# A two-block attention kernel: ternary weight pieces loaded and stored from ScalarE, and all seven quarters of the context kept in memory

## The chip, the cores and the metric

The kernel runs on one core of one Trainium2 chip. The metric is device time in microseconds (us) of one execution; lower is better. A core has five engines with a queue of instructions each: PE (TensorE, matrix products), DVE (VectorE), ACT (ScalarE), POOL (GpSimd) and SP (SyncE, here used for nothing but issuing DMAs). Semaphores hold an instruction back until what it needs is there, and what stands behind it in the same queue waits as well. On-chip data lie in SBUF (128 partitions) and in PSUM, into which PE writes its products. "In memory" below means DRAM outside both.

## The reference, cut to what matters

Eight sequences (B = 8) of 64 tokens of width 512 pass through two blocks. Each block lets the tokens attend to their sequence's context of 1601 rows of width 512, then to each other, then passes them through a feed-forward network; `n` is a layer norm. In short:

```python
x = x + cross_attention_0(n(x), ctx)      # 16 heads of 64, weights Wq, Wkv, Wout
x = x + spectral_attention_0(n(x))
x = x + moe_ffn_0(n(x))                   # 8 experts
x = x + cross_attention_1(n(x), ctx)      # 16 heads, weights Wq, Wk, Wv, Wp
x = x + attention_1(n(x))
x = x + ternary_ffn_1(n(x))
```

A cross attention is, for each sequence and head, `softmax(q @ k.T) @ v` with q from the tokens and k and v from the context. Block 0's is computed with the key weights multiplied onto the queries and the value weights applied after the mixing, so that the context itself stands in both large products. In the last network the two weight matrices (512x2048 and 2048x512) are rounded to three values, with one scale for each matrix:

```python
scale = 1.0 / clip(mean(abs(w)), 1e-05)
q = clip(round(w * scale), -1.0, 1.0) / scale
```

## The kernel before, in words

**The stages.** The program does block 0's cross attention (`l0_xattn`, 0 to about 1517 us of the span), its spectral attention, its experts (about 1600 to 1855), block 1's cross attention (`l1_xattn`, about 1855 to 2900), and block 1's attention with the ternary network (`l1_tail`, to the end). The change touches `l0_xattn`, a load in `l1_xattn`, and the class `TernaryWeights`, which the program makes ahead of the first stage.

**Order of instructions.** The kernel is written in one thread of program text. A scheduler of the language spreads it over the engines' queues and may move an instruction ahead of others of the same engine; the order in a queue is therefore not always that of the text. Buffers come from pools with a fixed number of copies, and a DMA into a buffer waits until the last reader of its former content is done.

**Block 0's cross attention.** It goes through 17 steps (the loop at L648). Step 2b + half does the scores of sequence b for eight of the 16 heads (`scores`, products at L468), and after them the mixing of the context rows by the weights of the step before (`attend`, products at L585, then v at L618). Scores need the context transposed, `ctxT`; mixing needs it by rows, `ctx`. Both are taken in six "pairs" of two tiles of 128 context rows; the last 65 rows are a tail, done apart (L461, L595). Every fourth step ends with `project_out` (L640).

**Seven products in place of eight.** A pair and its counterpart form a 2x2 block product, which is done in seven products on sums and differences of quarters. For the context's side, `Quarters.left` (L132 to L139) makes four such sums on POOL; a pair is therefore a tile of seven quarters, 128 x 7 x 256 f32 (917 KB), of which three hold plain quarters of the input and four the sums. `LEFT` says which quarter a product takes. All pairs, of scores and of mixing, come from one pool of six buffers (`cp`, tag "pair"), and the output weights in `project_out` use it as well. `Run.add` writes out the order of the seven products of one pair among those of the pair before, over the PSUM tags x, y and z with two buffers each; ACT copies the products p1, u2 and p5 out of PSUM (L428 in scores) and writes one sum with the bias (L447), DVE makes the other sums (L433). `softmax` works on DVE (L501, L508 to L515) and ACT (L502), while PE does the next scores.

**Loads and kept quarters.** `load_columns(b, keep)` loads the six pairs of ctxT for a step, each with two DMAs of 256 KB from the input (L183), and makes the four sums. In the first half of each sequence it also writes the four sums of each pair into DRAM tiles `kept[b]` (L189, 128 KB, and L190, 384 KB). In the second half the same quarters are loaded from the input again and the sums made again. `load_rows` loads ctx, also two DMAs a pair (L200). All these DMAs are issued by SP.

**Block 1's cross attention.** Its helper `load(b, g)` (L1430 to L1445) loads one group of two pairs (1.8 MB): from the input the plain quarters (two DMAs a pair), from `kept` the four sums (two DMAs a pair), so eight DMAs for a group, all from SP. The weight of its output projection is loaded at L1596, on SP too.

**The ternary weights.** They are cut into 16 pieces of 512 KB. `pass_by` (L1881) loads one into a buffer "piece" (two buffers). `measure` sums its absolute values on ACT (L1889); `scales` makes the two scales (L1893 to L1898); `round` loads the piece again, scales it and adds a constant that rounds (DVE, L1904), subtracts the constant on ACT with a bf16 result in a buffer "wq" (L1905, one buffer), clips it on DVE (L1906), and stores it to memory from SP (L1907), from where `l1_tail` loads it at the end of the program. In the program's text `aside(step)` (L363) measures two pieces at the end of each of the steps 2 to 9, makes the scales in step 10 and rounds three pieces at the end of each of the steps 10 to 15. In the trace the measures stand at 239 to 450 us and the rounds at 1015 to 1151 us.

Of the kernel before, what the change touches and what calls it, by code (L numbers as in the profile page):

```python
# [10 lines left out]
F32 = mybir.dt.float32  # L11
BF16 = mybir.dt.bfloat16
# [8 lines left out]
P = 128  # L21
# [102 lines left out]
class Quarters:  # L124
# [5 lines left out]

    LEFT = {1: 0, 2: 1, 3: 6, 4: 3, 5: 4, 6: 5, 7: 2}

    @staticmethod
    def left(nc, q):

        nc.gpsimd.tensor_add(q[:, 4, :], q[:, 2, :], q[:, 3, :])  # L136
        nc.gpsimd.tensor_sub(q[:, 5, :], q[:, 4, :], q[:, 0, :])
        nc.gpsimd.tensor_sub(q[:, 2, :], q[:, 0, :], q[:, 2, :])
        nc.gpsimd.tensor_sub(q[:, 6, :], q[:, 1, :], q[:, 5, :])  # L139


def l0_xattn(K, x, d, ternary, kept):
# [7 lines left out]
    with ExitStack() as es:  # L150
# [25 lines left out]

        def load_columns(b, keep=False):

            pairs = []
            for i in range(NPAIR):  # L180
                q = cp.tile([P, 7, QH], F32, tag="pair", name="ctxT")
                for j in range(2):
                    nc.sync.dma_start(  # L183
                        q[:, ds(2 * j, 2), :].rearrange("p h (c n) -> p (h c) n", n=P),
                        d["ctxT"][b, :, ts(2 * i + j, P)].rearrange("(c p) n -> p c n", p=P),
                    )
                Quarters.left(nc, q)
                if keep:
                    nc.sync.dma_start(kept[b][:, i, 3, :], q[:, 2, :])  # L189
                    nc.sync.dma_start(kept[b][:, i, 0:3, :], q[:, 4:7, :])  # L190
                pairs.append(q)
            return pairs

        def load_rows(b):

            pairs = []
            for i in range(NPAIR):
                q = cp.tile([P, 7, QH], F32, tag="pair", name="ctx")
                for j in range(2):
                    nc.sync.dma_start(  # L200
                        q[:, 0:4, :].rearrange("p (h j) n -> p j h n", j=2)[:, j],
                        d["ctx"][b, ts(2 * i + j, P), :].rearrange("p (h n) -> p h n", n=QH),
                    )
                Quarters.left(nc, q)
                pairs.append(q)
            return pairs
# [103 lines left out]
        load_tails(0)  # L310
        ctxT = load_columns(0, True)
        place = [tp.tile([P, 4, 3, QH], F32, tag="pt", name="stage").rearrange("p a b q -> p (a b q)") for _ in range(2)]
# [138 lines left out]
        def scores(b, qkt, ctxT):  # L451
# [12 lines left out]
            for i in range(NPAIR):  # L464

                def mul(ps, n, start, i=i):
                    for e in range(2):
                        nc.tensor.matmul(  # L468
                            ps,
                            lhsT=ctxT[i][:, Quarters.LEFT[n], ts(e, P)],  # L470
                            rhs=right[n][:, e, :],
                            start=start and e == 0,
                            stop=e == 1,
                            skip_group_check=not start,
                        )
# [94 lines left out]
        def attend(half, s, soft, ctx, o, first):  # L570
# [77 lines left out]
        for step in range(2 * B + 1):  # L648
            if step < 2 * B:
                b, half = divmod(step, 2)  # L650
                if step:
                    now, ctxT = queries_of(b, half), load_columns(b, half == 0)
# [749 lines left out]
def l1_xattn(K, x, d, ahead, queries_done, in_last, kept):  # L1402
# [7 lines left out]
    with ExitStack() as es:  # L1410
# [19 lines left out]
        def load(b, g):  # L1430

            q = cp.tile([P, 2, 7, QH], F32, tag="ctxT", name="ctxT")
            for u in range(2):
                i = 2 * g + u
                nc.sync.dma_start(
                    q[:, u, 0:2, :].rearrange("p h (c n) -> p (h c) n", n=P),
                    d["ctxT"][b, :, ts(2 * i, P)].rearrange("(c p) n -> p c n", p=P),
                )
                nc.sync.dma_start(
                    q[:, u, 3, :].rearrange("p (c n) -> p c n", n=P),  # L1440
                    d["ctxT"][b, SET:, ts(2 * i + 1, P)].rearrange("(c p) n -> p c n", p=P),
                )
                nc.sync.dma_start(q[:, u, 2, :], kept[b][:, i, 3, :])
                nc.sync.dma_start(q[:, u, 4:7, :], kept[b][:, i, 0:3, :])
            return q  # L1445
# [413 lines left out]
class TernaryWeights:  # L1859
# [26 lines left out]

    def measure(self, piece, i):
        w = self.pass_by(piece, i)
        self.nc.scalar.activation(w, w, AF.Abs, accum_out=self.part[:, i // 8, i % 8 : i % 8 + 1])  # L1889
# [9 lines left out]

    def round(self, piece, pool, i):  # L1900
        nc, n = self.nc, i // 8
        w = self.pass_by(piece, i)
        q = pool.tile([P, 1024], BF16, tag="wq", name="wq")
        nc.vector.tensor_scalar(w, w, self.scale[:, n : n + 1], MAGIC, ALU.mult, ALU.add)  # L1904
        nc.scalar.activation(q, w, AF.Identity, bias=self.down, scale=1.0)  # L1905
        nc.vector.tensor_scalar(q, q, 1.0, -1.0, ALU.min, ALU.max)  # L1906
        nc.sync.dma_start(self.to[i], self.shaped(q, i))  # L1907

# [493 lines left out]
```

## Time and profile before

| | |
|---|---|
| times of the three runs | 3087.1, 3088.03, 3089.5 us (median 3088.03) |
| the profiled execution | 3083.06 us, of which the span 3081.1 |
| mean granted PE clock of it | 0.987 |
| PE busy | 2980.5 us |
| POOL's sums of ctxT pairs, one of four lines (L136) | 96, mean 823 ns |
| a measure on ACT (L1889) | 1.06 us and 0.19 us for its sum |
| a round: DVE L1904, ACT L1905, DVE L1906 (medians) | 0.75, 1.15, 0.43 us |
| load of a piece, issue to landing (median) | 4.3 us |
| store of a rounded piece, issue to landing (median) | 3.6 us |

The profile is that of one execution. Busy shares are of the whole span. A row of the waits gives the waiting engine with its tile and line, what ended the wait, the total, how often, and the longest one. A row of a timeline gives the start, the duration, the engine, the line and the operation; "SPq" is SP's queue, where a row is the issuing of a DMA, not its transfer, and "x6" folds six of them into one row. "Granted clock" is the share of its full clock that PE was given in a stretch.

### The profile page before, as it was taken

To read this page: it belongs to the slowest core of one execution; us is meant where nothing else is said; L and a number is where in the kernel's file an instruction comes from. 1 tells how busy PE (TensorE), PEld (TensorE's weight loads), DVE (VectorE), ACT (ScalarE), POOL (GpSimd) and SP (SyncE) were. 2 spreads that over 40 slices of the span, in tenths; PEclk is the share of its full clock that TensorE was granted. 3 is DMA by queue.
4 is the path that set the end of the run, shared out by engine and by line. 5 is a ranking of instruction groups with operands and counts; after the bars stand their busy time and mean duration, and the time that the engine had idled before them with its cause. 6 is when DMAs were issued, how large, how long until landed. Compare 5 with 4: busy or idle time off the path is not lost.

```text
span 3081.1 us, 41104 instructions
## 1 busy us (share of the span) xinstructions
PE 2980.5 (97%) x15515; PEld 2288.4 (74%) x15521; DVE 1830.5 (59%) x3124; ACT 845.5 (27%) x1620; POOL 993.0 (32%) x959
## 2 busy tenths in 40 slices
PE   8999999999999989999999999999999999999887
PEld 7777778888888767888654446778788888888654
DVE  4845545666656656666433333578676676676746
ACT  2322241222222322222111222232332333323234
POOL 4434343544454534444110003221422413304000
PEclk9999999999999999999999999999999999999998
DMA  8265474434434564432659974302112022020260
GB/s 263 71 200 152 145 244 128 140 100 143 131 103 132 180 188 134 128 119 66 228 185 339 343 253 144 92 15 75 42 51 77 21 73 58 22 89 3 87 107 14
DMA packets 387187, 391.76 MB, mean 127 GB/s; under 512 B 55054, under 2 KB 289558, under 8 KB 385838
## 3 DMA queue, kind: packets, MB, share of 16 engines
q1 hardware_dynamic: 380761, 371.80, 39.2%
q10 hardware_dynamic: 5589, 15.24, 1.3%
q8 instruction: 123, 2.02, 0.3%
q0 software_dynamic: 640, 2.10, 0.2%
q14 instruction: 74, 0.61, 0.1%
HBM read 332.90 MB, written 56.16 MB: 126 GB/s over the span
## 4 chain that ended last, share of the span: by engine, by line
PE 58%; DVE 2%; ACT 1%; DMA 1%; issue 0%; POOL 0%; POOLq 0%; ACTq 0%; DVEq 0%; SPq 0%
PE x_ps L1528 11%; PE y_ps L1528 8%; PE s_ps L1691 6%; PE oe_ps L1231 4%; PE h_ps L1204 4%; PE acc L1742 3%; PE x_ps L585 3%; PE x_ps L468 2%; PE z_ps L585 2%; PE z_ps L468 1%; PE sum_ps L1575 1%; PE y_ps L585 1%; PE y_ps L468 1%; DMA wo<-in_L1x_Wp 1%; PE vt_ps L1619 1%; PE top_ps L1727 1%
## 5 line engine op out<-in xcount | busy, mean ns | idle before, releaser
L1588 POOL TENSOR_TENSOR r<-r,minus_half 128x52 f32<-128x52 f32 x32 | 276.9, 8673 | 558.0 <-DVE r L1587 558.0
L468 PE MATMUL x_ps<-qt,ctxT 128*128 128x256 f32 x1152 | 288.1, 384 | 9.6 <-ACT u L428 6.9
L585 PE MATMUL x_ps<-pt,ctx 128*128 128x256 f32 x1152 | 281.7, 382 | 7.2 <-DVE a L561 6.3
L468 PEld LDWEIGHTS x_ps<-qt,ctxT 128*128 128x128 f32 x1152 | 218.7, 192 | 50.4 <-ACT u L428 8.8
L585 PEld LDWEIGHTS x_ps<-pt,ctx 128*128 128x128 f32 x1152 | 217.3, 190 | 41.1 <-DVE a L561 6.5
L136 POOL TENSOR_TENSOR ctxT<-ctxT 128x256 f32<-128x256 f32 x96 | 79.0, 823 | 412.4 <-DMA ctxT<-in_ctxT 284.5
L1691 PE MATMUL s_ps<-qb,kT 128*128 128x256 f32 x832 | 201.2, 381 | 0.1
L449 DVE TENSOR_TENSOR m<-m,s 128x512 f32<-128x512 f32 x176 | 137.5, 781 | 95.8 <-ACT s L447 93.2
L136 POOL TENSOR_TENSOR ctx<-ctx 128x256 f32<-128x256 f32 x96 | 73.5, 765 | 348.5 <-DMA ctx<-in_ctx 275.4
L1691 PEld LDWEIGHTS s_ps<-qb,kT 128*128 128x128 f32 x832 | 154.2, 190 | 26.2 <-issue 3.5
L501 DVE TENSOR_TENSOR s<-s,top_ps 128x1024 f32<-128x1024 f32 (+1 forms) x112 | 123.2, 1135 | 23.3 <-PE top_ps L491 23.3
L1733 DVE TENSOR_TENSOR s<-s,top_ps 128x1792 f32<-128x1792 f32 x64 | 117.9, 1884 | 28.8 <-PE top_ps L1727 28.8
L433 DVE SCALAR_TENSOR_TENSOR s<-y_ps,bias,p 128x256 f32<-128x256 f32 x96 | 46.3, 483 | 146.2 <-PE y_ps L468 145.8
L1701 DVE TENSOR_TENSOR s<-s_ps,r 128x512 f32<-128x512 f32 x192 | 126.4, 682 | 10.8 <-PE s_ps L1691 10.2
L1734 ACT ACTIVATE s<-s 128x1792 f32<-128x1792 f32 x64 | 101.0, 1591 | 84.0 <-DVE s L1733 84.0
L1742 PEld LDWEIGHTS acc<-s,v 128*64 128x64 f32 x1664 | 96.1, 138 | 32.4 <-issue 27.0
L502 ACT ACTIVATE s<-s 128x1024 f32<-128x1024 f32 (+1 forms) x112 | 110.8, 996 | 30.0 <-DVE s L501 25.9
L1742 PE MATMUL acc<-s,v 128*64 128x128 f32 x1664 | 114.9, 280 | 4.1 <-ACT s L1734 4.1
L1204 PE MATMUL h_ps<-w,tok 128*128 128x512 f32 x256 | 117.3, 593 | 0.0
L1231 PE MATMUL oe_ps<-w,hT 128*128 128x512 f32 x256 | 115.6, 593 | 0.0
L515 DVE TENSOR_TENSOR total<-total,s 128x512 f32<-128x512 f32 x160 | 110.0, 687 | 3.5
L468 PE MATMUL x_ps<-qk,ctxT 128*128 128x256 f32 x384 | 104.9, 391 | 6.2 <-ACT s L447 4.0
(472 smaller groups left out, 6287.2 us busy)
## 6 DMA issues: line engine op xcount, KB each, us to landing
w<-in_L0f_W SPq DMA_DIRECT2D x64, 1024.0 KB, 5.8
ctxT<-in_ctxT SPq DMA_DIRECT2D x240, 256.0 KB, 4.7
ctx<-in_ctx SPq DMA_DIRECT2D x192, 256.0 KB, 3.4
kept<-ctxT SPq DMA_DIRECT2D x48, 384.0 KB, 2.8
ctxT<-kept SPq DMA_DIRECT2D x48, 384.0 KB
wvT<-in_L0x_WvT SPq DMA_DIRECT2D x16, 1024.0 KB, 8.4
qk<-qk_all SPq DMA_DIRECT2D x15, 1024.0 KB, 7.4
qk_all<-stage SPq DMA_DIRECT2D x32, 384.0 KB, 3.5
```

Of the source, the lines that this page charges most:

```text
L136: nc.gpsimd.tensor_add(q[:, 4, :], q[:, 2, :], q[:, 3, :])
L449: nc.vector.tensor_max(self.m, self.m if k else self.s[:, LAST, :], self.s[:, k, :])
L468: nc.tensor.matmul(ps, lhsT=ctxT[i][:, Quarters.LEFT[n], ts(e, P)], rhs=right[n][:, e, :], start=start and e == 0, stop=e == 1, skip_group ...
L501: nc.vector.tensor_sub(s[:, k : k + n], s[:, k : k + n], top.unsqueeze(1).to_broadcast([P, n, HALF]))
L585: nc.tensor.matmul(ps, lhsT=ctx[pair][:, Quarters.LEFT[n], ts(m, P)], rhs=right[n][:, i, :], start=start and i == 0, stop=i == 2, skip_gro ...
L1204: nc.tensor.matmul(ps, lhsT=self.tok[:, c, :], rhs=self.w1[n][:, c, :], start=c == 0, stop=c == DC - 1)
L1231: nc.tensor.matmul(ps, lhsT=self.hT[:, f, :], rhs=self.w2[f // 4][:, f % 4, :], start=f == 0, stop=f == 15)
L1528: nc.tensor.matmul(ps, lhsT=left(n, e), rhs=right(n, e), start=start and e == 0, stop=e == 1, skip_group_check=not start,)
L1588: nc.gpsimd.tensor_tensor(r, r, minus_half, ALU.pow)
L1691: nc.tensor.matmul(ps[:, i].rearrange("p h q -> p (h q)"), lhsT=kT[c][:, ts(k0 + i, P)], rhs=qb[c].rearrange("p h q -> p (h q)"), start=Tr ...
L1701: nc.vector.tensor_mul(out, ps, by)
L1742: nc.tensor.matmul(acc[ds(64 * j, 64), c, :], lhsT=v[:, k, ds(c * P + 64 * j, 64)], rhs=s[:, k, ts(j, P)], start=k == 0, stop=k == NK - 1,)
```

## The change

There are three edits.

1. In `l0_xattn`, `kept` holds all seven quarters of a pair. In the first half of a sequence the pairs are loaded and summed as before and then stored whole, one DMA a pair (917 KB), issued behind the loads of all six pairs. In the second half a pair is one DMA from `kept`, with no sums on POOL. `load_rows` splits its two DMAs by the halves of the columns and no longer by the two tiles of rows. The places of the quarters in a tile are renumbered (`LEFT`, `left`).
2. In `l1_xattn`, a group of two pairs is one DMA of 1.8 MB from `kept`.
3. The ternary pieces are loaded and stored by DMAs that ACT issues. The work on them becomes a generator, `of_weights`, started after step 3, of which `scores` and `attend` take one turn after each `run.add`: two loads, three turns with nothing, two measures, and so on; later two loads, four turns with nothing, two rounds. Rounding is done in the piece's own buffer: two f32 operations on DVE (scale and upper bound; lower bound and rounding constant), then ACT writes bf16 over the same buffer and issues the store.

```diff
-    LEFT = {1: 0, 2: 1, 3: 6, 4: 3, 5: 4, 6: 5, 7: 2}
+    LEFT = {1: 5, 2: 6, 3: 2, 4: 4, 5: 0, 6: 1, 7: 3}
...
-        def load_columns(b, keep=False):
+        def load_columns(b, half=0):
             pairs = []
             for i in range(NPAIR):
                 q = cp.tile([P, 7, QH], F32, tag="pair", name="ctxT")
-                for j in range(2):
-                    nc.sync.dma_start(
-                        q[:, ds(2 * j, 2), :].rearrange("p h (c n) -> p (h c) n", n=P),
-                        d["ctxT"][b, :, ts(2 * i + j, P)].rearrange("(c p) n -> p c n", p=P),
-                    )
-                Quarters.left(nc, q)
-                if keep:
-                    nc.sync.dma_start(kept[b][:, i, 3, :], q[:, 2, :])
-                    nc.sync.dma_start(kept[b][:, i, 0:3, :], q[:, 4:7, :])
+                if half:
+                    nc.sync.dma_start(q, kept[b][:, i])
+                else:
+                    for j in range(2):
+                        nc.sync.dma_start(
+                            q[:, ds(5 - 2 * j, 2), :].rearrange("p h (c n) -> p (h c) n", n=P),
+                            d["ctxT"][b, :, ts(2 * i + j, P)].rearrange("(c p) n -> p c n", p=P),
+                        )
+                    Quarters.left(nc, q)
                 pairs.append(q)
+            if not half:
+                for i, q in enumerate(pairs):
+                    nc.sync.dma_start(kept[b][:, i], q)
             return pairs
...
-        def aside(step):
-            if 2 <= step < 10:
-                for i in range(2):
-                    ternary.measure(piece, 2 * (step - 2) + i)
-            if step == 10:
-                ternary.scales(ps_m.tile([P, 16], F32, tag="mm", name="w_ps"), ones[:, 0:1])
-            if 10 <= step < 16:
-                for i in range(3 * (step - 10), min(3 * (step - 9), 16)):
-                    ternary.round(piece, zp, i)
+        def of_weights():
+            for i in range(0, ternary.PIECES, 2):
+                pieces = [ternary.pass_by(piece, i + j) for j in range(2)]
+                yield from (None,) * 3
+                for j in range(2):
+                    ternary.measure(pieces[j], i + j)
+                    yield
+            ternary.scales(ps_m.tile([P, 16], F32, tag="mm", name="w_ps"), ones[:, 0:1])
+            for i in range(0, ternary.PIECES, 2):
+                pieces = [ternary.pass_by(piece, i + j) for j in range(2)]
+                yield from (None,) * 4
+                for j in range(2):
+                    ternary.round(pieces[j], i + j)
+                    yield
+        aside = iter(())
...
                 run.add(mul, Scores(s, m, b, i))
                 some(2)
+                next(aside, None)
...
                     run.add(mul, Mixed(a, m, part == 0, tail))
                     some(2 * part)
+                    next(aside, None)
...
-            aside(step)
             if step == 3:
                 some(5 * NG)
+                aside = of_weights()
...
+        for _ in aside:
+            pass
...
         def load(b, g):
             q = cp.tile([P, 2, 7, QH], F32, tag="ctxT", name="ctxT")
-            for u in range(2):
...
+            nc.sync.dma_start(q, kept[b][:, ts(g, 2)])
             return q
...
     def pass_by(self, piece, i):
         w = piece([D], "wraw").rearrange("p a b -> p (a b)")
-        self.nc.sync.dma_start(self.shaped(w, i), self.from_[i])
+        self.nc.scalar.dma_start(self.shaped(w, i), self.from_[i])
         return w
...
-        q = pool.tile([P, 1024], BF16, tag="wq", name="wq")
-        nc.vector.tensor_scalar(w, w, self.scale[:, n : n + 1], MAGIC, ALU.mult, ALU.add)
+        q = w.bitcast(BF16)[:, :1024]
+        nc.vector.tensor_scalar(w, w, self.scale[:, n : n + 1], 1.0, ALU.mult, ALU.min)
+        nc.vector.tensor_scalar(w, w, -1.0, MAGIC, ALU.max, ALU.add)
         nc.scalar.activation(q, w, AF.Identity, bias=self.down, scale=1.0)
-        nc.vector.tensor_scalar(q, q, 1.0, -1.0, ALU.min, ALU.max)
-        nc.sync.dma_start(self.to[i], self.shaped(q, i))
+        nc.scalar.dma_start(self.to[i], self.shaped(q, i))
...
-        kept = [memory.tile([P, NPAIR, 4, QH], F32, tag=f"kept{b}", name="kept") for b in range(B)]
+        kept = [memory.tile([P, NPAIR, 7, QH], F32, tag=f"kept{b}", name="kept") for b in range(B)]
```

More of the change, by code (lines that the diff above doesn't have):

```diff
@@ L124 @@
 class Quarters:
-    LEFT = {1: 0, 2: 1, 3: 6, 4: 3, 5: 4, 6: 5, 7: 2}
+    LEFT = {1: 5, 2: 6, 3: 2, 4: 4, 5: 0, 6: 1, 7: 3}
     @staticmethod
     def left(nc, q):
[L136 to L139, printed above, removed]
+        nc.gpsimd.tensor_add(q[:, 0, :], q[:, 3, :], q[:, 4, :])
+        nc.gpsimd.tensor_sub(q[:, 1, :], q[:, 0, :], q[:, 5, :])
+        nc.gpsimd.tensor_sub(q[:, 3, :], q[:, 5, :], q[:, 3, :])
+        nc.gpsimd.tensor_sub(q[:, 2, :], q[:, 6, :], q[:, 1, :])
 def l0_xattn(K, x, d, ternary, kept):
@@ L198, in load_rows @@
                 q = cp.tile([P, 7, QH], F32, tag="pair", name="ctx")
-                for j in range(2):
+                for h in range(2):
                     nc.sync.dma_start(
-                        q[:, 0:4, :].rearrange("p (h j) n -> p j h n", j=2)[:, j],
-                        d["ctx"][b, ts(2 * i + j, P), :].rearrange("p (h n) -> p h n", n=QH),
+                        q[:, ds(5 - 2 * h, 2), :],
+                        d["ctx"][b, ts(i, 2 * P), ts(h, QH)].rearrange("(j p) n -> p j n", p=P),
                     )
@@ L310, in l0_xattn @@
         load_tails(0)
-        ctxT = load_columns(0, True)
+        ctxT = load_columns(0)
         place = [tp.tile([P, 4, 3, QH], F32, tag="pt", name="stage").rearrange("p a b q -> p (a b q)") for _ in range(2)]
@@ L651, in l0_xattn @@
                 if step:
-                    now, ctxT = queries_of(b, half), load_columns(b, half == 0)
+                    now, ctxT = queries_of(b, half), load_columns(b, half)
                     if half == 0:
@@ L1432, in load @@
             q = cp.tile([P, 2, 7, QH], F32, tag="ctxT", name="ctxT")
-            for u in range(2):
[L1434 to L1444, printed above, removed]
+            nc.sync.dma_start(q, kept[b][:, ts(g, 2)])
             return q
@@ L1885, in shaped, with measure @@
         return w if i < 8 else w.rearrange("p (c n) -> p c n", n=D)
-    def measure(self, piece, i):
-        w = self.pass_by(piece, i)
+    def measure(self, w, i):
         self.nc.scalar.activation(w, w, AF.Abs, accum_out=self.part[:, i // 8, i % 8 : i % 8 + 1])
@@ L1898, in scales, with round @@
         nc.vector.reciprocal(self.scale, self.size)
-    def round(self, piece, pool, i):
+    def round(self, w, i):
         nc, n = self.nc, i // 8
-        w = self.pass_by(piece, i)
-        q = pool.tile([P, 1024], BF16, tag="wq", name="wq")
-        nc.vector.tensor_scalar(w, w, self.scale[:, n : n + 1], MAGIC, ALU.mult, ALU.add)
+        q = w.bitcast(BF16)[:, :1024]
+        nc.vector.tensor_scalar(w, w, self.scale[:, n : n + 1], 1.0, ALU.mult, ALU.min)
+        nc.vector.tensor_scalar(w, w, -1.0, MAGIC, ALU.max, ALU.add)
         nc.scalar.activation(q, w, AF.Identity, bias=self.down, scale=1.0)
-        nc.vector.tensor_scalar(q, q, 1.0, -1.0, ALU.min, ALU.max)
-        nc.sync.dma_start(self.to[i], self.shaped(q, i))
+        nc.scalar.dma_start(self.to[i], self.shaped(q, i))
     def load1(self, pool):
```

## The prediction

> **What bounds the kernel now.** I read the page first: busy shares, the chain that ended last, the costliest groups, the DMA issues.
>
> ```profile
> PE 2980.5 (97%) x15515; PEld 2288.4 (74%) x15521; DVE 1830.5 (59%) x3124; ACT 845.5 (27%) x1620; POOL 993.0 (32%) x959
> ...
> PE 58%; DVE 2%; ACT 1%; DMA 1%; issue 0%; POOL 0%; POOLq 0%; ACTq 0%; DVEq 0%; SPq 0%
> ...
> L136 POOL TENSOR_TENSOR ctxT<-ctxT 128x256 f32<-128x256 f32 x96 | 79.0, 823 | 412.4 <-DMA ctxT<-in_ctxT 284.5
> ...
> ctxT<-in_ctxT SPq DMA_DIRECT2D x240, 256.0 KB, 4.7
> ```
>
> The reader is to see that TensorE (PE) is busy 97% of the span and carries the chain. POOL, SP's queue and most transfers are not on it. So the 192 sums that POOL loses and the DMAs that SP loses are worth nothing as such; all that a change can win here is idle time of PE. So I next asked what PE waited for in the first attention (0 to 1520 us), then what ACT waited for while the ternary pieces are rounded (1000 to 1160 us), and then SP's timeline there. In the first two the columns are: total us, times, longest us.
>
> ```profile
> PE x_ps L468 <- ACT u L428: 6.9, 4, 4.9
> ...
> PE x_ps L585 <- DVE a L561: 6.3, 1, 6.3
> PE y_ps L468 <- DVE s L433: 4.1, 1, 4.1
> PE x_ps L468 <- ACT s L447: 4.0, 4, 1.9
> ...
> PE x_ps L468 <- DMA ctxT<-in_ctxT: 2.2, 1, 2.2
> ```
>
> ```profile
> ACT wq L1905 <- DMA w_out<-wq: 38.3, 11, 17.6
> ```
>
> ```profile
> 1083.80 4.76 SPq L183 DMA_DIRECT2D ctxT<-in_ctxT  x6
> ...
> 1099.04 0.32 SPq L190 DMA_DIRECT2D kept<-ctxT  x1
> 1099.45 0.38 SPq L1907 DMA_DIRECT2D w_out<-wq  x1
> ```
>
> These join up. The clipped piece was ready at 1083.8 (L1906 starts 1083.33 and lasts 0.43), but SP works in order and stood at the context's loads and kept stores: its store (L1907) went out 15.7 us later. The next round on ACT (L1905) waited 17.6 us for that store's landing, attention's copies stood behind it on ACT and the sums behind those on DVE, and PE idled 6.34 us from 1097.75. The same happens at 1124.62 (4.93 us; the store left at 1121.86). In PE's timeline the gaps that the change can reach are:
> - Start (steps 0 to 1): 1.21 + 1.75 + 2.21 + 4.09 = 9.26 us.
> - Measures (239 to 450 us): 0.86 + 1.17 + 1.85 + 0.64 = 4.5 us, and 3.4 us at half clock from 422.0, which loses 1.7: 6.2 us.
> - Rounds (1015 to 1150): 0.93 + 0.98 + 0.55 + 6.34 + 4.93 + 0.96 = 14.7 us. The granted clock is 0.5 for 6.8 us from 1101.3 and from 1128.6; PE had work for 4.0 and 5.9 us of these, so half of 9.9 is lost: 4.9. Together 19.6 us.
> - Second attention: 0.75 + 0.67 + 1.13 = 2.55 us, at the loads of its output weight (L1596), which stand on SP behind eight loads of a group.
> In all some 38 us, 1.2% of the span. Undisturbed steps take 84.6 us each (L585 starts its x_ps at 1261.06, 1345.68, 1430.40 in the chain).
>
> **The change part by part**, against the profiled run's own 3083.06 us (span 3081.1).
>
> Start. In the built order the first x_ps matmul of step 1 no longer stands ahead of the top_ps matmuls (L491), so the 2.21 us in which it held PE come earlier for the softmax behind it. The 4.09 us gap waits for a sum on DVE (L433) while DVE works through softmax; two of DVE's operations there took 1.49 us beside POOL's sums against 0.95 elsewhere, and step 1 has no POOL sums now: 2 x 0.54 = 1.1. I take -2.2 - 1.1 = **-3.3**. Bounds: all 9.26 and the half-clock time after it gone, -14; or 4.7 MB more (2.36 MB more stores in step 0, 2.36 MB more loads in step 1) at the 0.30 MB/us that the busiest 10-us slices there moved (309 to 347 GB/s) come wholly ahead of step 1, +15.7. I choose near the good end because the slices from 80 us on are nearly empty (146, 14, 0 GB/s) and step 1 needs the pairs one by one, 6.05 us of PE each; one pair is 0.92 MB, 3.1 us at that rate.
>
> Kept quarters elsewhere: **0**. Hidden behind the 84.6 us of PE of a step: a step's DMA share in the undisturbed steps is 0.43 and 0.31, and 2.36 MB more add 8 us at 0.30 MB/us. If that cover were gone in all 14 steps that remain it would be 110 us, but no steady step has PE waiting on a context load, so I keep none of it but rival 4. POOL's 192 sums x 0.82 = 158 us lie beside PE: 0. Stores now stand on SP behind all loads of the batch, which brings loads forward and delays none that PE waited for.
>
> Second attention: one issue in place of eight (2214.40 to 2218.3 us, 3.9 us on SP) lets the output weight's load go some 3.4 us earlier, but its transfer then runs beside the 1.8 MB of the group; I take **-0.75**, bounds -2.55 (all of it) and +2 (the transfer is late by some half of its 4 us).
>
> Measures. Each piece is now loaded by ACT itself: 16 issues (an ACT issue of a DMA took 0.33 to 0.44 us in the expert stage), and the ACT operation (1.06 + 0.19) waits for landing (issue to landing of these loads: median 4.3 us). In the built order all 16 are packed into the end of step 3 and step 4, as tightly as before, not one in each step. The wait that is added stands at the head of ACT's queue with the copies of p1, u2, p5 behind it, and they have 3.46, 1.73 and 2.59 us of PE work as cover. Old waits for ACT go, new ones come: **+1**, bounds -6 (all hidden) and +8 (two uncovered remainders of 4.3 - 1.73 and one of half-clock windows of 3).
>
> Rounds. SP's delay of the stores (15.7 and more) is gone: ACT issues the store right after its own operation. But ACT's queue now holds: load, load, round, round, store, store; each reload waits for its buffer's store to land (store issue to ACT going on took 4.2 us: 1018.70 to 1022.98, 1025.24 to 1029.31), and each round for the load and two DVE operations. A cycle of two pieces is 4.3 (load) + 1.5 (two f32 operations of 0.75) + 1.15 (ACT) + 4.2 (store) + 0.7 (issues) + 1.5 (second piece) = 13.4 us, against 12.1 us of PE for two pairs. The built order puts all 16 rounds into step 8 (with the output projection 84.6 + 6.2 = 90.8 us of PE) and the start of step 9, eight cycles: 107 us. In the scores of step 8 some three cycles overrun their pairs and put p5 and u2 copies behind a landing: 4 to 8 us. First part of attend: 1.5. In the second part rounds stand on DVE ahead of the sums that PE waits for: 5. In step 9 the p5 copy stands behind the last round: 4.6. Half clock after the longer gaps: 2 to 3. Together 17 to 21, I take 17.6 against the 19.6 of before: **-2**. Bounds: -15 (ACT's idle 73% takes nearly all of it) and +15 (every one of eight cycles holds a copy by some 4.3 us). DVE's 16 x (1.5 - 1.18) = 5 us lie beside PE.
>
> Weighing rules: the trace has 4.3 us from issue to landing for the pieces that SP issues, and none that ACT issues. The Trainium skill, "DMA: Bandwidth & Descriptors", section "Issuing engines are not separate DMA queues", says that issuing from several engines saves only the issuing time; by that, moving these DMAs to ACT would be worth about 0 in transfer, and the waits of ACT would be pure loss. The trace shows a gain the rule leaves out, 15.7 us of a store standing behind SP's other work. Another: PE got half clock at 422.0 after a gap of 1.85 us. "TensorE: Matmul & The Clock Gate", "What's actually happening", has the clock fall after an idle window of about 3.4 us; by it the measures of before would be 4.5, not 6.2, and the shorter gaps after the change would cost no clock, the sum 2 to 3 us lower. I go by the row.
>
> Sum: -3.3 + 0 - 0.75 + 1 - 2 = **-5.05**; 3083.06 - 5 = 3078. The median of the three runs stands 5.0 above the profiled one, so on its scale 3088.03 - 5 = **3083**.
>
> **Rivals** (differences from before; 0.2% is 6.2 us, about what a measurement here tells from no change).
> 1. Forecast: old stalls go, new ones of like size come on ACT: -13 to +4, chance 0.40. For: 13.4 against 12.1, and all rounds in one step.
> 2. The ternary stream hides nearly wholly: -3.3 - 0.75 - 3 (measures) - 14 (rounds) = -21, from -13 to -35, so 3067. For: ACT is 27% busy, and SP's 15.7 us were the longest wait. Against: ACT's queue is in order. Chance 0.22.
> 3. Slower: ACT's in-order queue. A landing of 4.2 or 4.3 us at its head, twice a cycle, holds a copy that has 1.73 to 3.46 us of cover; it decides once more than some five of the eight cycles do so. Rounds +12, measures +4, start and weight -4: +12 (+5 to +35), 3100. For: the trace's own 6.34 and 4.93 us gaps are this mechanism. Chance 0.30.
> 4. The kept traffic comes late at the start or in first halves: +6 to +16, 3099. Chance 0.08.
> 5. That it does not do what it says is part of 1 and 3: "one operation a step" is not what the built order shows, so the stream stays as dense as it was.
>
> **How the numbers follow.** Faster by over 0.2%: 0.42 of case 1 (0.17) and all of 2 (0.22): 0.39. Within: the rest of case 1 (0.23) and a little of 3 (0.01): 0.24. Slower: 0.29 + 0.08 = 0.37. The range leaves out the lower part of 2 (under -23, 0.09) and the upper part of 3 (over +16, 0.11): 3065 to 3104; case 1's own is 3075 to 3092.
>
> **What would show it.** Right: no wait of ACT for a store over 5 us; PE gaps in step 8 and at the start of step 9 of 2 to 5 us that end on ACT or DVE, 17 us or so in all; the gap near 91 us at 1 to 2 us; every other step 84.6 us. Wrong: step 8 without gaps (case 2), gaps in every pair of it or a clock of 0.5 through it (case 3), PE waiting for ctxT in second halves or at step 1 (case 4).

## The result and the profile after

The change makes no difference that can be measured: a median of 3088.93 us over 20 runs against 3087.91 for the kernel before, also over 20, a ratio of 1.0006 (95% interval 0.9998 to 1.0013). The profiled execution has a span of 3083.9 us against 3081.1. The forecast was 3083, about 5 us less, and its likeliest case was that old stalls go and new ones of like size come. That is what happened, but two of the sums have other sizes than forecast, and they cancel. To a time within 0.2% of before the prediction gave a chance of 0.24, less than to faster (0.39) or to slower (0.37).

The page of the changed kernel, the lines that answer to those of before:

```profile
PE 2982.0 (97%) x15515; PEld 2289.8 (74%) x15521; DVE 1823.7 (59%) x3124; ACT 846.3 (27%) x1620; POOL 843.3 (27%) x767
...
PE 89%; DMA 4%; DVE 3%; ACT 2%; issue 1%; POOL 0%; SPq 0%; ACTq 0%; POOLq 0%; DVEq 0%
...
kept<-ctxT SPq DMA_DIRECT2D x48, 896.0 KB
...
ctxT<-in_ctxT SPq DMA_DIRECT2D x96, 256.0 KB
```

(The profile's KB are of 1024 bytes: 896.0 KB are the 917 KB of a pair.) POOL is busy 150 us less, and the DMAs of 256 KB that load ctxT from the input fell from 240 to 96. None of it shows in the time; it stood beside PE. The chains can't be compared share by share: the shares of the one before sum to 62%, as it could be followed back only to about 1130 us, and this one's sum to 99%. But it shows where to look: 4% of the span, DMAs that something on the chain waited for, and 3% DVE.

To find where the time went, I read from PE's timeline when each step of the first attention reaches its first `top_ps` matmul. Column k below is the time from that of step k-1 to that of step k, so column 8 holds the scores of step 8, and column 9 the mixing of step 8, its output projection and the scores of step 9. An undisturbed column is 84.6 us, or 91.4 with an output projection. The first column starts at 0 and ends at step 1's matmul, the second ends at step 5's. "Second attention" runs from the last transpose of the experts' hidden values to the first matmul of the last of the four output projections. The rows marked e are experiments told below; all is in us:

| profile | 0-1 | 2-5 | 8 | 9 | 11 | 12 | second attention |
|---|---|---|---|---|---|---|---|
| before | 128.4 | 413.4 | 84.6 | 91.5 | 89.1 | 103.2 | 1061.1 |
| changed | 123.6 | 415.1 | 99.8 | 107.6 | 84.6 | 84.6 | 1057.6 |
| changed, again (e11) | 124.3 | 416.1 | 98.6 | 106.4 | 84.6 | 84.6 | 1059.8 |
| kept edits alone (e1) | 124.3 | 412.9 | 84.6 | 91.4 | 88.5 | 93.5 | 1057.6 |
| ternary edits alone (e2) | 127.5 | 416.1 | 96.1 | 101.6 | 84.8 | 85.1 | 1061.9 |
| halves from input (e5) | 125.2 | 419.6 | 99.2 | 100.8 | 85.0 | 84.6 | 1057.7 |
| loads from SP (e6) | 124.2 | 410.7 | 100.0 | 97.4 | 84.6 | 84.6 | 1058.7 |
| spread (e3) | 123.5 | 409.2 | 86.1 | 91.7 | 84.7 | 86.4 | 1063.0 |

The rounds cost the kernel before 4.5 us in column 11 and 18.6 in column 12, 23 in all. In the changed kernel those two are clean, and columns 8 and 9 hold 15.2 and 16.2 us, 31 in all. The start won 4.8, the second attention 3.5; columns 2 to 5, with the measures, lost 1.7. The waits of PE in columns 8 and 9 (columns: total us, times, longest):

```profile
PE z_ps L479 <- ACT p L439: 7.6, 2, 5.3
PE m_ps L498 <- DVE m L460: 4.3, 1, 4.3
PE x_ps L479 <- ACT p L439: 2.8, 1, 2.8
PE x_ps L597 <- DVE a L573: 2.6, 1, 2.6
PE x_ps L479 <- DVE s L444: 2.3, 2, 2.1
PE x_ps L479 <- ACT u L439: 1.3, 1, 1.3
```

Of these, 11.7 us end on ACT and, with one more wait of 0.5 us, 9.7 on DVE. Here is one wait of each kind. On ACT, this is its timeline in step 8:

```profile
764.19 0.33 ACTq L1909 DMA_DIRECT2D w_out<-wraw  x1
764.56 0.37 ACT L439 COPY p<-x_ps 128x256 f32<-128x256 f32 x1 [0.40 <-PE x_ps L479]
769.95 0.34 ACTq L1885 DMA_DIRECT2D wraw<-in_L1f_w1T  x1
770.33 0.37 ACT L439 COPY p<-z_ps 128x256 f32<-128x256 f32 x1 [5.39 <-DMA w_out<-wraw]
```

The reload of a buffer (L1885) waits for the store of its old content to land. It stands in ACT's queue, so ACT stands idle for 5.39 us with the copy of p5 behind it, whose product PE had finished at about 766, and PE idles 2.26 us from 768.58. On DVE, at the end of the scores of step 8:

```profile
799.46 0.69 DVE L1907 TENSOR_SCALAR wraw<-wraw 128x1024 f32<-128x1024 f32 x1
802.99 1.22 DVE L1906 TENSOR_SCALAR wraw<-wraw,wscale 128x1024 f32<-128x1024 f32 x1 [2.83 <-DMA wraw<-in_L1f_w1T]
804.13 1.21 DVE L460 TENSOR_TENSOR m<-m,s 128x512 f32<-128x512 f32 x1
```

Here a round (L1906) waits for its load; the last maximum of the scores (L460) stands behind it, and PE, which needs that for the transposes of m, waits 4.34 us. The gaps of PE over 0.4 us in columns 8 and 9 sum to 21.2 us. The rest of the 31 is mostly clock: it was at half for 20.5 us in four stretches (from 771.0, 805.2, 849.5 and 870.0 us), PE had work for 14.9 us of them, and half of that, some 7.4, is lost. It shows in these two windows (busy us of PE, PEld, DVE, ACT and POOL, then the granted clock, the DMA share and GB/s):

```profile
711.00:795.00 84.00, 78.08 (x394) 64.22 (x393) 55.09 (x90) 23.77 (x41) 36.09 (x46) 0.98 0.56 186
795.00:880.00 85.00, 69.37 (x329) 53.36 (x328) 52.66 (x82) 23.27 (x33) 11.56 (x12) 0.90 0.66 227
```

### The profile page after: what moved, and what is told of

The parts are those of the page before. It is cut to its first block, busy times and chain, and to the rows that moved or that the text cites. A ratio compares the mean times of both kernels' runs of the same rounds, so it can differ in the third digit from the quotient of the medians.

```text
span 3083.9 us, 40425 instructions
## 1 busy us (share of the span) xinstructions
PE 2982.0 (97%) x15515; PEld 2289.8 (74%) x15521; DVE 1823.7 (59%) x3124; ACT 846.3 (27%) x1620; POOL 843.3 (27%) x767
## 4 chain that ended last, share of the span: by engine, by line
PE 89%; DMA 4%; DVE 3%; ACT 2%; issue 1%; POOL 0%; SPq 0%; ACTq 0%; POOLq 0%; DVEq 0%
PE x_ps L1532 11%; PE x_ps L597 10%; PE x_ps L479 10%; PE y_ps L1532 8%; PE s_ps L1695 6%; PE z_ps L479 5%; PE z_ps L597 5%; PE oe_ps L1246 4%; PE h_ps L1219 4%; PE acc L1746 3%; PE y_ps L597 3%; PE y_ps L479 2%; PE s_ps L472 2%; DMA wraw<-in_L1f_w1T 1%; PE qk_ps L257 1%; PE v_ps L631 1%
## 5 line engine op out<-in xcount | busy, mean ns | idle before, releaser
L460 DVE TENSOR_TENSOR m<-m,s 128x512 f32<-128x512 f32 x176 | 133.4, 758 | 94.6 <-ACT s L458 91.8
L1746 PEld LDWEIGHTS acc<-s,v 128*64 128x64 f32 x1664 | 96.1, 138 | 32.4 <-issue 27.0
L479 PE MATMUL z_ps<-qk,ctxT 128*128 128x256 f32 x384 | 101.4, 387 | 9.4 <-ACT p L439 9.4
## 6 DMA issues: line engine op xcount, KB each, us to landing
kept<-ctxT SPq DMA_DIRECT2D x48, 896.0 KB
ctxT<-kept SPq DMA_DIRECT2D x48, 896.0 KB
```

The lines of the kernel that those rows point to most:

```text
L460: nc.vector.tensor_max(self.m, self.m if k else self.s[:, LAST, :], self.s[:, k, :])
L479: nc.tensor.matmul(ps, lhsT=ctxT[i][:, Quarters.LEFT[n], ts(e, P)], rhs=right[n][:, e, :], start=start and e == 0, stop=e == 1, skip_group ...
L1746: nc.tensor.matmul(acc[ds(64 * j, 64), c, :], lhsT=v[:, k, ds(c * P + 64 * j, 64)], rhs=s[:, k, ts(j, P)], start=k == 0, stop=k == NK - 1,)
```

## The experiments

My theory A after this comparison: the two parts of the change add up; the ternary stream on ACT costs 31 us because work of attention stands behind its DMA waits in the in-order queues of ACT and DVE, and the kept edits save some 8. Rival B: the larger kept traffic makes the stream dear. Ratios are to the kernel before, run on the same chip beside each; the ranges in brackets are 95% intervals.

**e1, the kept edits alone** (`aside`, `measure` and `round` as before):

```diff
-                if keep:
-                    nc.sync.dma_start(kept[b][:, i, 3, :], q[:, 2, :])
-                    nc.sync.dma_start(kept[b][:, i, 0:3, :], q[:, 4:7, :])
+                if half:
+                    nc.sync.dma_start(q, kept[b][:, i])
...
+            if not half:
+                for i, q in enumerate(pairs):
+                    nc.sync.dma_start(kept[b][:, i], q)
```

> The edits on the kept quarters alone; the ternary stream as in the kernel before. Theory A (the two halves of the change add up: the kept quarters save some 5 us in steps 0 to 1 and 3.5 us in the second attention, and the ternary stream on ACT gives it back, because ACT and DVE hold attention's copies and sums behind its DMA waits): 8 us less than before, the rounds costing about 23 us as before (steps 11 and 12 together 192 us where two undisturbed ones take 169). Rival B (the kept traffic is what makes the rounds dear: more megabytes on the same DMA engines, so that loads and stores of pieces land late): the rounds cost 30 us or more here too, and the time is that of before or above. Rival C (the gain at the start is no more than chance of one profile): no change, within 2 us.

Measured: 3066.84 us, ratio 0.9944 (0.9924 to 0.9963), so 17 us less, 11 to 24 by the interval. Twice what theory A gave, and against rival B. The table shows why: 4.1 at the start and 3.5 in the second attention as said, but the rounds on SP cost 3.9 + 8.9 = 13 us in place of 23 in this profile. SP's timeline of this run, in the stretch where the kernel before held a store for 15.7 us:

```profile
1077.96 3.95 SPq L186 DMA_DIRECT2D ctxT<-in_ctxT  x6
1086.47 6.02 SPq L194 DMA_DIRECT2D kept<-ctxT  x3
1092.54 0.43 SPq L1899 DMA_DIRECT2D w_out<-wq  x1
...
1102.71 6.49 SPq L194 DMA_DIRECT2D kept<-ctxT  x3
1109.25 0.44 SPq L579 DMA_DIRECT2D wvT<-in_L0x_WvT  x1
1109.73 1.84 SPq L203 DMA_DIRECT2D ctx<-in_ctx  x2
1111.61 0.70 SPq L1899 DMA_DIRECT2D w_out<-wq  x1
```

The two stores go out at 1092.54 and 1111.61, where the kernel before had 1099.45 and 1121.86. This kernel runs 4.9 us ahead by then, so they are 2 and 5 us earlier in their step, and the long gaps of 6.34 and 4.93 us are one of 3.50. So the kept edits had themselves removed nearly half of what moving the stream off SP was to remove. That it is the order of the kept stores on SP which does it is read from this one timeline; the other parts of the edit (the split of `load_rows`, the renumbering) are in this run too and were not tried alone.

**e2, the ternary edits alone** (the loads, sums and stores of the context as before; diff as in the change).

> The ternary edits alone; context loads, sums and kept stores as in the kernel before. Theory A: rounds cost 31 us as in the changed kernel in place of 23, measures 2 more: 8 to 11 us above the kernel before. Rival B: without the larger traffic the rounds on ACT cost 20 us or less: 3 us under the kernel before or better.

Measured: 3089.82 us, ratio 1.0003 (0.9991 to 1.0015): no difference. Neither forecast holds. The rounds cost 11.5 + 10.2 = 22 us in this profile, against 23 on SP and 31 in the changed kernel (29 in e11). So the stream on ACT is about as dear as it was on SP, and the kept edits make it dearer: rival B has a part. Theory A's sum of two parts fails too, since -17 and +1 make -16 and the whole change gives +2.

**e3, the stream spread over the steps.** In the built order of the change all 16 rounds stand in step 8 and the start of step 9. Here each load and each round is tied to its step by data: a one-element copy of the last pair's scores (`anchor[0]`) into the buffer ahead of the load, and a scale made on DVE as 0 times the maxima so far (`anchor[1]`) plus the scale. The mixing takes no turns any more, so all of the stream stands in scores: two rounds in each of the steps 8 to 15.

```diff
+                    nc.scalar.copy(w[0:1, 0:1], anchor[0][0:1])
+                    nc.scalar.dma_start(ternary.shaped(w, i + j), ternary.from_[i + j])
...
-                yield from (None,) * 4
-                for j in range(2):
-                    ternary.round(pieces[j], i + j)
-                    yield
...
+                    nc.vector.scalar_tensor_tensor(
+                        now, anchor[1], 0.0, ternary.scale[:, n : n + 1], ALU.mult, ALU.add
+                    )
+                    ternary.round(pieces[j], i + j, now)
+                yield from (None,) * 3
...
-                    next(aside, None)
```

> The changed kernel with its ternary stream tied to the steps: a tiny ACT copy from the step's scores into the buffer ahead of each load, and the round's scale made from the step's maxima, so that the scheduler can't pull them ahead; two pieces measured twice in each of the steps 4 to 7 and two rounded in each of the steps 8 to 15, each load three pairs ahead of its use. Theory A: no reload stands behind a store any more and no round behind a load, so nearly all of the 31 us and the measures' 2 go: 25 to 33 us less than the changed kernel. Rival B: loads still land late beside the kept traffic, and the stream keeps half its cost: 10 to 16 us less.

Measured: 3058.8 us, ratio 0.9906 (0.9888 to 0.9925): 29 us under the kernel before, some 31 under the changed one, as theory A has it. From the start of column 8 to the end of step 16 it takes 791.2 us against 815.1 in the changed kernel. PE's waits from 710 to 1450 us:

```profile
PE x_ps L497 <- DVE s L462: 3.8, 4, 1.1
PE m_ps L518 <- DVE m L478: 1.9, 4, 0.6
PE z_ps L497 <- ACT p L457: 1.1, 4, 0.3
```

No wait is longer than 1.1 us. The pieces, the 48 DMAs from ACT and the kept traffic are the same. What is gone is that a reload follows a store, and a round a load, within a few microseconds: in step 8 the loads go out at 747.72 and 748.24, the first round starts at 769.38, the stores leave at 773.08 and 775.29, and the next load comes in the next step's scores, at 840.62. With that the pieces also share the DMA engines with fewer of their own kind at a time; this run can't part the two.

**e4, no stream.**

```diff
+            nc.gpsimd.memset(w, 0.0)
+            nc.gpsimd.memset(ternary.part, 1.0)
+            for i in range(ternary.PIECES):
+                nc.scalar.dma_start(ternary.to[i], ternary.shaped(w.bitcast(BF16)[:, :1024], i))
             ternary.scales(ps_m.tile([P, 16], F32, tag="mm", name="w_ps"), ones[:, 0:1])
```

> The changed kernel without the measuring and rounding of the ternary weights: zeros are stored in place of the rounded pieces by 16 DMAs from ACT after step 3, and the two scales come from ones. It gives the floor, what the stream costs in all. Theory A and rival B both: 31 to 36 us less than the changed kernel. If it is under 20 less, the long steps 8 and 9 have another cause than the stream.

Measured: 3060.52 us, ratio 0.9908 (0.9887 to 0.9929), 30 us under the changed kernel by the ratios, where 31 to 36 were expected. It leaves out the network's rounded weights, so it is a measure of time only. By the totals e3 is at this floor: nearly all of the 30 us that the stream costs the changed kernel are its waits. By the stages the spread rounds still cost something: from column 8 to the end of step 16 it takes 784.9 us here, 6 less than in e3. Columns 2 to 5 take 412.9, 4 more than in e3; this kernel stores its zeros there, and the cause of the 4 us stays open.

**e5, second halves from the input** (contention, with the order of the queues otherwise kept):

```diff
-                if half:
-                    nc.sync.dma_start(q, kept[b][:, i])
-                else:
+                if True:
                     for j in range(2):
...
                     Quarters.left(nc, q)
```

> The changed kernel, but second halves load their pairs from the input again and make the sums on POOL again; all seven quarters are still stored, and the second attention still loads them. It tells whether the rounds on ACT cost 31 us in the changed kernel and 22 us in the ternary edits alone because of the larger loads of the second halves (5.5 MB in place of 3.1 in step 9). Theory A (the order of the queues sets the cost, and the difference of the two is the larger traffic in steps 8 and 9): step 9 falls from 107.6 to about 102 us, step 8 stays near 99; at the start the 2 to 4 us that were won come back; in all 0 to 4 us under the changed kernel. Theory B (the traffic has no part in it; the order of instructions alone): step 9 stays at 107 and the time is 3 us above the changed kernel.

Measured: 3085.23 us, ratio 1.0000 (0.9988 to 1.0011). The total can't tell it from the changed kernel, but column 9, with the loads of a second half, falls from 107.6 (106.4 in e11) to 100.8, and column 8 stays at 99.2, as theory A has it. Columns 2 to 5 take 419.6, 4.5 more than in the changed kernel, which is why the total does not show it. So a second half that loads 5.5 MB from `kept` makes the rounds beside it 6 to 7 us dearer. ACT's timeline of the changed kernel there, and that of e5:

```profile
857.21 0.35 ACTq L1909 DMA_DIRECT2D w_out<-wraw  x1
857.65 1.15 ACT L1908 ACTIVATE wraw<-wraw,wdown 128x1024 bf16<-128x1024 f32 x1 [0.48 <-DVE wraw L1907]
858.83 0.34 ACTq L1909 DMA_DIRECT2D w_out<-wraw  x1
864.87 3.20 ACTq L1885 DMA_DIRECT2D wraw<-in_L1f_w2T  x2
868.11 0.69 ACT L473 ACTIVATE s<-s_ps,bias 128x512 f32<-128x512 f32 x1 [9.31 <-DMA w_out<-wraw]
```

```profile
860.01 0.34 ACTq L1907 DMA_DIRECT2D w_out<-wraw  x1
860.63 1.15 ACT L1906 ACTIVATE wraw<-wraw,wdown 128x1024 bf16<-128x1024 f32 x1 [0.65 <-DVE wraw L1905]
861.81 0.35 ACTq L1907 DMA_DIRECT2D w_out<-wraw  x1
866.00 1.53 ACTq L1883 DMA_DIRECT2D wraw<-in_L1f_w2T  x2
```

Two stores leave, and each of the two reloads waits for the store of its own buffer. In the changed kernel the reloads go out at 864.87 and 867.61, 7.7 and 8.8 us after their stores; in e5 6.0 and 5.3 us after. From 860 to 870 us the DMA engines moved 392 GB/s in the changed kernel and 329 in e5. Their busy share was 1.01 and 1.05, so the share alone does not tell the two apart. That it is the larger loads which delay the landings is the likely reading, not shown beyond these two profiles.

**e6, loads of the pieces from SP**, stores from ACT:

```diff
-        self.nc.scalar.dma_start(self.shaped(w, i), self.from_[i])
+        self.nc.sync.dma_start(self.shaped(w, i), self.from_[i])
```

> The changed kernel with the loads of the pieces issued by SP again; stores stay on ACT. Theory A (a reload that waits for its buffer's store to land, standing on ACT ahead of attention's copies, makes about half of the 31 us; the other half is DVE's in-order wait for the load): the gaps that end on ACT in step 8 and at the start of step 9 go, and the time falls by 8 to 16 us. Rival (the reload's wait then holds SP's context loads, as in the kernel before, and the landing is no earlier for DVE): within 5 us of the changed kernel.

Measured: 3075.86 us, ratio 0.9971 (0.9959 to 0.9983): 9 us under the kernel before, 11 under the changed one, as theory A has it. PE's waits in columns 8 and 9:

```profile
PE x_ps L479 <- DVE s L444: 10.2, 3, 5.9
PE x_ps L597 <- DVE a L573: 3.1, 1, 3.1
PE m_ps L498 <- DVE m L460: 0.6, 1, 0.6
```

Every wait on ACT is gone (11.7 us in the changed kernel) and those on DVE have become 13.9 from 9.7. Column 8 stays at 100.0, where waits on DVE took the place of those on ACT; column 9 falls by 10, to 97.4. So the reload on ACT's queue is worth about 10 us. A round that waits on DVE for its load is the other part, and issuing the loads from SP did not remove it: the rounds still cost 15.4 + 6.0 = 21 us.

**e7, the spread stream in the kernel before** (e3's diff without the kept edits), and **e8, the spread version with its DMAs on SP**:

```diff
-                    nc.scalar.dma_start(ternary.shaped(w, i + j), ternary.from_[i + j])
+                    nc.sync.dma_start(ternary.shaped(w, i + j), ternary.from_[i + j])
...
-        nc.scalar.dma_start(self.to[i], self.shaped(q, i))
+        nc.sync.dma_start(self.to[i], self.shaped(q, i))
```

> The kernel before with the ternary stream of the spread version, and none of the kept edits. Theory A (the kept edits are worth what they save outside the stream, some 4 us at the start and 3.5 in the second attention, once the stream waits nowhere): 18 to 23 us under the kernel before, 6 to 9 above the spread version. Rival (the kept edits are worth the 17 to 20 us that they saved alone): 8 to 12 us under the kernel before.

> The spread version with loads and stores of the pieces issued by SP. Theory A (what counts is how far apart a piece's load, rounding, store and reload stand, not which engine issues): within 4 us of the spread version. Rival (issuing from ACT is itself worth something, because SP's stores stand behind context loads): 8 us or more above it, with PE gaps after late stores.

Measured: e7 3059.66 us, ratio 0.9918 (0.9904 to 0.9933); e8 3057.34, ratio 0.9912 (0.9896 to 0.9927). e8 answers as its theory A has it: with the pieces spread, the issuing engine makes no difference that these runs can tell. e7 is 25 us under the kernel before, more than theory A's 18 to 23 and far more than its rival's 8 to 12, and within the intervals of e3 and e8: nearly the whole gain is in the spreading.

**e9 and e10, e8's stream with the two rounds of a step two pairs apart**, with and without the kept edits; and **e11, the changed kernel once more**:

```diff
                     ternary.round(pieces[j], i + j, now)
-                yield from (None,) * 3
+                    if j == 0:
+                        yield from (None,) * 2
+                yield
```

> The spread version on SP, with the two rounds of a step two pairs apart, so that one piece at a time passes DVE; kept edits in. Theory A: the gaps of 0.6 to 1.1 us that end on DVE's sums in the steps with rounds shrink, 0 to 4 us under the spread versions, some 28 to 32 us under the kernel before. Rival (those gaps come from elsewhere): the same as the spread versions within 2 us.

> The same stream without the kept edits (context loads, sums and stores of the kernel before). It prices the kept edits when no stall of the stream is left to help or harm. Theory A: what the changed kernel's profile saves outside the stream, 4.8 us at the start and 3.6 in the second attention: 6 to 9 us above the version with kept edits. Rival B' (larger traffic takes back what the start saves): within 3 us of it.

> The changed kernel once more, for a second profile. If steps 8 and 9 take 99 to 100 and 106 to 109 us again, their length is the kernel's and not one execution's; if either moves by more than 3 us, sums made from one profile are no better than that.

Measured: e9 3058.94 us, ratio 0.9913 (0.9900 to 0.9926): the split gains nothing over e8 that can be told, and PE still has waits of up to 1.0 us on DVE's sums (4.8 us in seven), so two rounds in a row were not their cause. e10 3067.68, ratio 0.9928 (0.9913 to 0.9943), 4.6 us above e9 by the ratios, between both forecasts; e7 is 1.9 above e8. The kept edits are worth 2 to 5 us once the stream stalls nothing, but both pairs' intervals overlap, so it stays open whether they are worth anything; the start is 4.1 us shorter in e9's profile and the second attention 1.3. e11 took 3093.34 us; columns 8 and 9 are 98.6 and 106.4, within 1.2 us of the first profile, so their length belongs to the kernel.

The spread versions e3, e8 and e9 beat both kernels by 0.9%. They can't be told apart, nor can e7, without the kept edits, be told from them.

## Why the prediction was right, point by point

The time came out within 6 us of the forecast, but in part by luck. The stalls were of the kind and in the places that the prediction named; the rounds cost 10 us more than its sum had, and the start and the second attention gave back 4 us more than it had. The prediction's own terms:

- **Start, -3.3**: measured -4.8, and -4.1 in e11. The mechanism held: step 1 has no `x_ps` ahead of `top_ps` any more, the two operations on DVE took 0.95 us each, and the gap of 4.09 us is 3.16. The gaps over half a microsecond fell from 9.26 to 6.77 us, 2.5 less. The rest fits the clock, which was not in the -3.3: it was at half for 13.7 us of this stretch before and for 3.4 after (6.8 in e11).
- **Kept quarters elsewhere, 0**: right in undisturbed steps (84.6 before, 84.6 to 85.0 after). As a term of the sum it was wrong in two ways. "Stores now stand on SP behind all loads of the batch" was priced at nothing and is worth 10 us to a stream that SP issues (e1), which the changed kernel can't use, as its stream has left SP. And the cover hides the loads from PE, but not from the rounds, which became 6 to 7 us dearer in column 9 (e5).
- **Second attention, -0.75**: measured -3.5 in the first profile, -1.3 in e11. All three waits for the output weight (2.55) were gone in the first, and one of 0.8 us was left in e11; I had counted a third of them as gone. Over all profiles this stage took 1057.6 to 1063.0 us with the kept edits and 1061.1 to 1062.7 without, so the term can't be had more exactly.
- **Measures, +1**: measured +1.7 over columns 2 to 5, and +2.7 in e11.
- **Rounds, -2**: this term was off by its size. Measured +8, from 23 to 31. I had 19.6 for the rounds of before, as I summed gaps over half a microsecond; by the length of the steps it was 23. For after I had 17.6. The terms that I listed add up to 17.1 to 22.1, not 17 to 21, and their middle is the 19.6 of before, so the -2 was a choice near the good end. The sites were right: rounds packed in step 8 and the start of 9, reloads on ACT behind landings, rounds on DVE behind loads. The gaps were 21.2 where I had some 15, and the clock some 7 where I had 2 to 3. Moving the stream to ACT by itself cost about nothing, 22 against 23 (e2); most of the +8 came with the larger kept traffic, which I had priced at 0.
- **The two errors against each other**: -5 was forecast for the whole in the profile and +2.8 measured. The columns' own terms sum to -4.8 + 1.7 + 8.2 - 3.5 = +1.6; the other 1.2 lie in the remaining steps and stages, one profile against another.
- **Rival 3**, ACT's in-order queue with +12 for the rounds, is near what the rounds alone show (+8), though e2 has most of that from the traffic. **Rival 5**, that the edit does not do what it says, was the key: "one operation a step" was not in the built order, and e3, which makes it true, takes off 31 us. I had said so and given it no time of its own. **Rival 2**, the stream hidden wholly (-21), is what the spreading then gave, and more (-29 in e3); its reason, that ACT is 27% busy, was of no use by itself.
- **What would show it**: "no wait of ACT for a store over 5 us" did not hold (5.39 and 9.31). Gaps of 2 to 5 us, 17 or so in all, were to stand in step 8 and at the start of 9: they sum to 21.2, the longest 5.35. The gap near 91 us came to 3.16, not 1 to 2. None of the signs of the rivals came: step 8 has gaps, but not in every pair, and PE waits for no ctxT there or at step 1.
- **The rules weighed**: by the Trainium skill, "DMA: Bandwidth & Descriptors", section "Issuing engines are not separate DMA queues", issuing DMAs from several engines saves only the time of issuing. With the stream spread the runs agree: e8 and e3 differ by under 2 us. With the stream packed they do not: e6 differs from the changed kernel by 11 us by nothing but the engine that issues the loads, because the wait ahead of a DMA blocks the queue it stands on. By the Trainium skill, "TensorE: Matmul & The Clock Gate", section "What's actually happening", the clock falls after an idle window of about 3.4 us. Here shorter gaps were enough: in the changed kernel it was at half for about 3.4 us from 771 us on, after a gap of 2.26, as the row at 422 us had it in the kernel before after one of 1.85. But no half clock followed the gap of 2.10 us that ended at 779.18, so the length of a gap alone did not decide it either.

## What to carry to other kernels

Work that is to fill an engine's idle time costs by its waits, not by its duration: a DMA or a consumer that waits for another DMA's landing holds everything queued behind it on its engine, so a load, its use, the store and the next reload should stand further apart than a landing takes. In e3 a round stood 22 us behind its load, where the median landing took 4.2 us; how near they may stand was not tried. Spreading such work in the text of a program did not spread it in the queues, as the scheduler pulled it ahead; look at the built order and tie the work to its step by data. And two edits that lean on the same queue don't add up: -17 and +1 made +2 here, because one of them had already removed nearly half of the stall that the other was for (e1), and put load on the DMA engines that the other came to depend on (e5).

## What the runs showed that I had not expected

- Gaps cost about a third as much again in clock: in columns 8 and 9 of the changed kernel 21.2 us of gaps came with some 7.4 us lost to half clock, and became 31 us of time. The granted clock was 0.90 from 795 to 880 us.
- One profile carries some 5 us that belong to no edit: from the expert gate's logits to the first transpose of the experts' hidden values took 51.5 to 54.1 us in eleven profiles and 56.2 and 56.9 in e2 and e10, and the end of the program after the second attention 170.8 to 177.4 us. The lengths of undisturbed steps of the first attention agreed within half a microsecond or so, so differences of some microseconds there can be read from single profiles.
